# Attention convolutions with taps and channels stacked to 128 rows, their inputs kept as padded maps in DRAM

One core of one Trainium2 chip runs the whole program. The metric is the device time of one execution in microseconds (us); lower is better. The kernel before takes 12191.53 us (median of four runs, 12184.75 to 12194.58).

## The reference, cut to what matters

The program takes four images of 96 channels by 128 x 128 pixels through two layers. The first is a state-space layer (four directional scans). The second, to which the change belongs, splits its normalised input into a positive half x1 and a negative half x2 and runs this on them:

```python
def _relu_split_norm(x, ...):                 # per image: mean, counts, variances, then
    ...                                       # x1 = scale1*relu(x)+shift1 where x>0, else 0 (as built)
    return (out, sc1 * x1 + x1n, sc2 * x2 + x2n)

def _attn_conv(x1, x2, aw1, aw2, aw3):        # C = 96, K = 3, kk = 9, pad = 1
    key = _unfold_nonoverlap(_conv2d(x1, aw1, pad), K).reshape(B, C, kk, -1)
    qry = _unfold_nonoverlap(_conv2d(x2, aw2, pad), K).reshape(B, C, kk, -1)
    attn = jnp.einsum('bckl,bqkl->bqck', key, qry)
    attn = softmax(attn.reshape(B, C, C * kk) / sqrt(C * kk), axis=2)
    w_attn = attn.reshape(B, C, C, K, K)      # a 3x3 convolution kernel for each image
    value = _conv2d(x1, aw3, pad)
    return jax.vmap(lambda v, w: _conv2d(v[None], w, pad)[0])(value, w_attn)

y1 = _layer_norm(_attn_conv(x1, x2, aw1, aw2, aw3))
y2 = _layer_norm(_conv2d(x2, w_conv2, K // 2)) * x1
```

So there are five 3x3 convolutions of 96 to 96 channels for each image: keys and queries (needed only as 3x3 patches), value ("v"), the plain one ("c"), and the last with the softmax weights ("apply").

## The kernel before

An image's normalised input `X` lies in SBUF. Strips of nine rows are made from it, one half at a time, with a border of zeros. Each convolution is nine matmuls with 96 rows, one for a tap, over three image rows (384 columns). Keys and queries are 15 matmuls whose stationary operand is the image (126 patch positions), copied by VectorE to unit step first.

```python
def make_half(dst, src, side, scale, shift):            # ACT scales, DVE masks
    nc.scalar.activation(dst, src, AF.Identity, scale=..., bias=...)
    nc.vector.scalar_tensor_tensor(dst, src, 0.0, dst, ALU.is_le if side else ALU.is_gt, ALU.mult)

def strip(t, side):
    xs = p2.tile([C, 13, W + 2], F32, name="xs")
    # ... memsets of the border ...
    make_half(xs[:, a:e, 1 : W + 1], src, side, scale, shift)      # src: rows of X in SBUF
    x5 = p2.tile([C, 5, 3, 4, NI], F32, name="x5")                 # NI = 42
    by3 = xs[:, 0:12].rearrange("p (i r) w -> p r i w", r=3)
    for sw in range(5):
        nc.vector.tensor_copy(x5[:, sw], by3[:, :, :, sw : sw + 3 * NI - 2 : 3])
    return xs, x5

def unfolded(x5, w, name, bufs):          # 3 groups of 15 matmuls; lhsT = x5[:, sw, ...] (96x126, unit step)
    ...
def conv(xs, w, r, n):
    pc = ps.tile([C, 3, W], F32, name="pc")
    for t in range(KK):                   # KK = 9
        dh, dw = divmod(t, 3)
        nc.tensor.matmul(pc[:, :n], lhsT=w[:, t], rhs=xs[:, r + dh : r + dh + n, dw : dw + W], ...)
    return pc

for t in range(NST):                      # NST = 14 strips of ST = 9 rows
    xs1, x51 = strip(t, 0)
    key = unfolded(x51, ws[0], "key", 2)
    # ... v convolution of the strip into vpad (SBUF, padded) ...
    xs2, x52 = strip(t, 1)
    qry = unfolded(x52, ws[1], "qry", 1)
    # ... key x query matmuls, c convolution to DRAM ...
# attn_apply: 32 chunks of nine matmuls over 512 columns of vpad, weights watT from SBUF
```

In the scan of the first layer, a small input `xr` comes by DMA for every two steps:

```python
def front(n):
    xr = p2.tile([KS, 2 * SN], BF16, name="xr", bufs=3)
    for a, img in enumerate(imgs):
        nc.sync.dma_start(xr[a * KI : (a + 1) * KI], xsp[img][k][:, sl])
    # ... pd = wdt x xr (TensorE), softplus and exp (ACT) ...
```

Of the kernel before, what the change touches and what calls it, by code (L numbers as in the profile page):

```python
# [32 lines left out]
KW = 3 * C  # L33
ROWS = (0, 2, 1, 3)
# [13 lines left out]
def kernel(  # L48
# [67 lines left out]
    def filled(value, name):  # L116
        t = const.tile([C, C], F32, name=name, tag=name)
        nc.vector.memset(t, value)
        return t
# [3 lines left out]
    mean192 = filled(1.0 / (2 * C), "mean192")  # L123
    eps = const.tile([C, 1], F32, name="eps", tag="eps")
# [205 lines left out]
    def ssm_scan(zs, xsp, yms):  # L330
# [6 lines left out]
        with (  # L337
# [26 lines left out]
            def front(n):  # L364
# [6 lines left out]
                xr = p2.tile([KS, 2 * SN], BF16, name="xr", bufs=3)  # L371
# [254 lines left out]
    def attn_maps(p1, X, vpad, scale, shift, c2d):  # L626



        watT = p1.tile([C, KK, C], F32, name="watT")  # L630
        c2st = p1.tile([C, NST * 3 + 1, 6], F32, name="c2st")
        with (
            tc.tile_pool(name="w1", bufs=1) as pw,
            tc.tile_pool(name="d2", bufs=2) as p2,
            tc.tile_pool(name="dps", bufs=2, space=PSUM) as ps,
        ):
            ws = []
            for name, src in (("k", aw1), ("q", aw2), ("v", aw3), ("c", w_conv2)):
                t = pw.tile([C, KK, C], F32, name=f"w_{name}")
                nc.sync.dma_start(t, src)  # L640
                ws.append(t)
            nc.gpsimd.memset(vpad[:, 0 : H + 2 : H + 1, :], 0.0)
            nc.gpsimd.memset(vpad[:, 1 : H + 1, 0 : W + 2 : W + 1], 0.0)


            pa = ps.tile([C, 2, 512], F32, name="pa", bufs=1)

            def strip(t, side):
                r0 = t * ST
                n = 13 if t == NST - 1 else 12  # L650
                xs = p2.tile([C, 13, W + 2], F32, name="xs")
                lo, hi = max(r0 - 1, 0), min(r0 - 1 + n, H)
                a, e = lo - (r0 - 1), hi - (r0 - 1)
                nc.gpsimd.memset(xs[:, :n, 0 : W + 2 : W + 1], 0.0)  # L654
                if a > 0:
                    nc.gpsimd.memset(xs[:, 0], 0.0)
                if e < n:
                    nc.gpsimd.memset(xs[:, e:n], 0.0)
                src = X[:, lo * W : hi * W].rearrange("p (h w) -> p h w", w=W)
                make_half(xs[:, a:e, 1 : W + 1], src, side, scale, shift)  # L660

                x5 = p2.tile([C, 5, 3, 4, NI], F32, name="x5")
                by3 = xs[:, 0:12].rearrange("p (i r) w -> p r i w", r=3)
                for sw in range(5):
                    nc.vector.tensor_copy(x5[:, sw], by3[:, :, :, sw : sw + 3 * NI - 2 : 3])  # L665
                return xs, x5

            def unfolded(x5, w, name, bufs):

                m = p2.tile([3 * NI, KK, C], F32, name=name, bufs=bufs)  # L670
                for kh in range(3):
                    pk = ps.tile([3 * NI, KW], F32, name="pk")
                    order = [(dh, sw) for dh in range(3) for sw in (2, 0, 1, 3, 4)]
                    for n, (dh, sw) in enumerate(order):
                        sh = kh + dh
                        k0, k1 = max(0, sw - 2), min(2, sw)
                        at = dh * 3 + 2 - sw + k0
                        nc.tensor.matmul(  # L678
                            pk[:, k0 * C : (k1 + 1) * C],
                            lhsT=x5[:, sw, sh % 3, sh // 3 : sh // 3 + 3].rearrange(  # L680
                                "p i j -> p (i j)"
                            ),
                            rhs=w[:, at : at + k1 - k0 + 1].rearrange("p t o -> p (t o)"),
                            start=(n == 0),
                            stop=(n == len(order) - 1),
                        )
                    nc.scalar.copy(
                        m[:, kh * 3 : kh * 3 + 3].rearrange("p t o -> p (t o)"), pk
                    )
                return m  # L690

            def conv(xs, w, r, n):
                pc = ps.tile([C, 3, W], F32, name="pc")
                for t in range(KK):
                    dh, dw = divmod(t, 3)
                    nc.tensor.matmul(  # L696
                        pc[:, :n],
                        lhsT=w[:, t],
                        rhs=xs[:, r + dh : r + dh + n, dw : dw + W],
                        start=(t == 0),  # L700
                        stop=(t == KK - 1),
                    )
                return pc

            for t in range(NST):
                chunks = [(0, 3), (3, 3), (6, 3)] + ([(9, 2)] if t == NST - 1 else [])
                xs1, x51 = strip(t, 0)
                key = unfolded(x51, ws[0], "key", 2)
                for r, n in chunks:
                    pc = conv(xs1, ws[2], r, n)  # L710
                    row = t * ST + r + 1
                    nc.vector.tensor_copy(vpad[:, row : row + n, 1 : W + 1], pc[:, :n])  # L712
                xs2, x52 = strip(t, 1)
                qry = unfolded(x52, ws[1], "qry", 1)
                for k in range(KK):
                    nc.tensor.matmul(
                        pa[:, k // 5, (k % 5) * C : (k % 5 + 1) * C],
                        lhsT=qry[:, k],
                        rhs=key[:, k],
                        start=(t == 0 and k in (0, 5)),  # L720
                        stop=(t == NST - 1 and k in (4, 8)),
                    )
                for i, (r, n) in enumerate(chunks):
                    pc = conv(xs2, ws[3], r, n)
                    cc = p2.tile([C, 3 * W], F32, name="cc")
                    nc.scalar.copy(cc[:, : n * W], pc[:, :n].rearrange("p h w -> p (h w)"))  # L726
                    nc.vector.bn_stats(c2st[:, t * 3 + i], cc[:, : n * W])  # L727
                    at = (t * ST + r) * W
                    nc.sync.dma_start(c2d[:, at : at + n * W], cc[:, : n * W])


            sm = p2.tile([C, KK, C], F32, name="sm", tag="qry", bufs=1)
            nc.vector.tensor_copy(
                sm[:, 0:5].rearrange("p t o -> p (t o)"), pa[:, 0, : 5 * C]
            )
            nc.scalar.copy(sm[:, 5:9].rearrange("p t o -> p (t o)"), pa[:, 1, : 4 * C])
            flat = sm.rearrange("p t o -> p (t o)")
            s = 1.0 / math.sqrt(C * KK)
            mx = col("mx")
            nc.vector.reduce_max(mx, flat, AX.X)  # L740
            nc.vector.tensor_scalar(mx, mx, -s, None, ALU.mult)
            den = col("den")
            nc.scalar.activation(flat, flat, AF.Exp, scale=s, bias=mx, accum_out=den)
            nc.vector.reciprocal(den, den)
            nc.vector.tensor_scalar(flat, flat, den, None, ALU.mult)
            for k in range(KK):
                pT = ps.tile([C, KW], F32, name="pk")
                nc.tensor.transpose(pT[:, :C], sm[:, k], ident)
                nc.vector.tensor_copy(watT[:, k], pT[:, :C])  # L749
        return watT, c2st  # L750

    def attn_apply(p1, vpad, watT, od):

        ost = p1.tile([C, NCH, 6], F32, name="ost")
        with (
            tc.tile_pool(name="e3", bufs=3) as p3,
            tc.tile_pool(name="eps", bufs=4, space=PSUM) as ps,
        ):
            for c in range(NCH):
                po = ps.tile([C, R, W], F32, name="poc")  # L760
                for t in range(KK):
                    dh, dw = divmod(t, 3)
                    nc.tensor.matmul(  # L763
                        po,
                        lhsT=watT[:, t],
                        rhs=vpad[:, c * R + dh : c * R + dh + R, dw : dw + W],
                        start=(t == 0),
                        stop=(t == KK - 1),
                    )
                oc = p3.tile([C, CH], F32, name="oc")  # L770
                nc.scalar.copy(oc, po.rearrange("p h w -> p (h w)"))
                nc.vector.bn_stats(ost[:, c], oc)
                nc.sync.dma_start(od[:, bass.ts(c, CH)], oc)
        return ost
# [153 lines left out]
```

## Time and profile before

The stages are read from the first and last record of each kind in the trace: a scan from the first to the last of GpSimd's sums into `y`; the wait from the last coefficient of the split to the first attention matmul; the maps stage from there to the first transpose of the softmax weights; the transition from there to the first apply matmul; apply to its last matmul; the end to the last matmul of the output stage (`pf`). The scan runs twice, the rest four times.

| stage, kernel before | us each | times |
|---|---|---|
| scan | 1047.9 | 2 |
| wait for the first attention matmul | 4.1 | 4 |
| maps (keys, queries, v, c) | 930.9 | 4 |
| transition to apply | 3.2 | 4 |
| apply | 247.4 | 4 |
| end | 166.0 | 4 |

How the page shows that TensorE bounds the maps and apply stages is told in the prediction below, with its lines.

### The profile page before, as it was taken

To read this page: it belongs to the slowest core of one execution; us is meant where nothing else is said; L and a number is where in the kernel's file an instruction comes from. 1 tells how busy PE (TensorE), PEld (TensorE's weight loads), DVE (VectorE), ACT (ScalarE), POOL (GpSimd) and SP (SyncE) were. 2 spreads that over 40 slices of the span, in tenths; PEclk is the share of its full clock that TensorE was granted. 3 is DMA by queue.
4 is the path that set the end of the run, shared out by engine and by line. 5 is a ranking of instruction groups with operands and counts; after the bars stand their busy time and mean duration, and the time that the engine had idled before them with its cause. 6 is when DMAs were issued, how large, how long until landed. Compare 5 with 4: busy or idle time off the path is not lost. (4 is left out here: it accounts for less than half of the span.)

```text
span 12183.9 us, 75678 instructions
## 1 busy us (share of the span) xinstructions
PE 9313.2 (76%) x29184; PEld 4477.1 (37%) x29184; DVE 4792.4 (39%) x4422; ACT 3083.6 (25%) x3474; POOL 2677.1 (22%) x1557
## 2 busy tenths in 40 slices
PE   6949655564999874999879496555649998759998
PEld 2313211112766323775223132111227762236752
DVE  1010088876222375221410101888752213752215
ACT  0000166734111123110200002667331112231102
POOL 1000099940000110000200001999300002100003
PEclk9979855566999876999789797555669998769997
DMA  1030212221000230000210302222300002300003
GB/s 40 27 69 27 67 59 73 83 93 31 8 7 10 64 111 15 8 7 13 87 49 27 71 26 78 62 70 71 99 24 7 8 11 73 108 7 8 8 14 95
DMA packets 256745, 552.66 MB, mean 45 GB/s; under 512 B 69210, under 2 KB 86518, under 8 KB 249216
## 3 DMA queue, kind: packets, MB, share of 16 engines
q1 hardware_dynamic: 231840, 472.09, 13.7%
q0 software_dynamic: 24544, 75.73, 2.1%
q8 instruction: 230, 3.77, 0.1%
q14 instruction: 131, 1.07, 0.0%
HBM read 306.33 MB, written 241.17 MB: 45 GB/s over the span
## 5 line engine op out<-in xcount | busy, mean ns | idle before, releaser
L271 PE MATMUL pz<-xs,weff 97*96 97x512 f32 x4608 | 2018.0, 596 | 14.7 <-DVE xs L256 14.7
L271 PEld LDWEIGHTS pz<-xs,weff 97*96 97x96 f32 x4608 | 741.8, 163 | 1285.7 <-issue 1208.6
L401 PE MATMUL pB<-xr,wbc 60*128 60x512 bf16 (+1 forms) x768 | 387.6, 599 | 1012.1 <-DVE h L439 595.0
L448 POOL TENSOR_TENSOR y<-y,t 128x1024 f32<-128x1024 f32 x384 | 1041.8, 2715 | 61.3 <-DVE t L443 58.5
L419 POOL TENSOR_TENSOR t<-dl,u 128x1024 f32<-128x1024 f32 x384 | 998.0, 2605 | 244.1 <-DMA u<-zs 214.6
L696 PE MATMUL pc<-xs,w_v 96*96 96x384 f32 (+1 forms) x3096 | 1013.5, 487 | 19.0 <-DVE xs L622 19.0
L696 PE MATMUL pc<-xs,w_c 96*96 96x384 f32 (+1 forms) x3096 | 1000.2, 482 | 0.0
L763 PE MATMUL poc<-vpad,watT 96*96 96x512 f32 x2304 | 989.8, 592 | 1.7 <-DVE watT L749 1.7
L678 PE MATMUL pk<-w_k,x 96*126 96x96 f32 (+2 forms) x5040 | 856.4, 334 | 3.0 <-DVE x L665 3.0
L678 PEld LDWEIGHTS pk<-w_k,x 96*126 96x126 f32 x5040 | 795.2, 199 | 84.5 <-issue 8.4
L654 POOL MEMSET xs<- 96x24 f32 (+1 forms) x112 | 14.1, 128 | 3588.9 <-PE pc L696 3313.3
L678 PE MATMUL pk<-w_q,x 96*126 96x96 f32 (+2 forms) x5040 | 801.3, 320 | 0.0
L401 PEld LDWEIGHTS <-wbc 60*128 60x128 bf16 (+1 forms) x1536 | 189.7, 124 | 1649.8 <-issue 1427.0
L678 PEld LDWEIGHTS pk<-w_q,x 96*126 96x126 f32 x5040 | 747.6, 189 | 70.6 <-issue 8.4
L293 DVE COPY xn<-px 32x512 f32<-32x512 f32 x128 | 86.6, 676 | 1717.4 <-PE px L289 1717.4
L278 ACT ACTIVATE z<-pz,dwb 96x512 f32<-96x512 f32 x256 | 174.9, 683 | 2031.6 <-PE pz L271 2031.6
L696 PEld LDWEIGHTS pc<-xs,w_v 96*96 96x96 f32 x3096 | 503.0, 164 | 494.9 <-issue 491.5
L696 PEld LDWEIGHTS pc<-xs,w_c 96*96 96x96 f32 x3096 | 498.4, 162 | 471.3 <-issue 467.2
L712 DVE COPY vpad<-pc 96x384 f32<-96x384 f32 (+1 forms) x172 | 94.8, 551 | 1355.7 <-PE pc L696 1355.7
L727 DVE BATCH_NORM_STATS2 c2st<-cc 96x6 f32<-96x384 f32 (+1 forms) x172 | 95.1, 553 | 1339.9 <-ACT cc L726 1339.9
L424 DVE TENSOR_TENSOR pB<-t,pB 128x1024 f32<-128x1024 f32 x384 | 471.0, 1227 | 361.9 <-POOL t L419 341.6
L328 ACT ACTIVATE dl<-pd,dtb 128x512 f32<-128x512 f32 x768 | 491.9, 684 | 428.1 <-PE pd L380 419.9
(186 smaller groups left out, 10788.4 us busy)
## 6 DMA issues: line engine op xcount, KB each, us to landing
xr<-xsp SPq DMA_DIRECT2D x256, 240.0 KB
zs<-z POOLq DMA_DIRECT2D x128, 384.0 KB, 3.4
u<-zs SPq DMA_DIRECT2D x96, 512.0 KB
yms<-y SPq DMA_DIRECT2D x96, 512.0 KB
yc<-yms SPq DMA_DIRECT2D x128, 384.0 KB
xsp<-piece SPq DMA_DIRECT2D x144, 192.0 KB
xr<-in_x SPq DMA_DIRECT2D x32, 768.0 KB
xc<-in_x SPq DMA_DIRECT2D x128, 192.0 KB
```

Of the source, the lines that this page charges most:

```text
L271: nc.tensor.matmul(pz, lhsT=weff[:, t, j * C : (j + 1) * C], rhs=xs[:, q * R + dh : q * R + dh + R, dw : dw + W], start=(t == 0), stop=(t ...
L278: nc.scalar.activation(z[:, j], pz.rearrange("p h w -> p (h w)"), AF.Silu, bias=dwb[:, j : j + 1],)
L328: nc.scalar.activation(dst, src, AF.Softplus, bias=bias)
L401: nc.tensor.matmul(p[:, j : j + CH], lhsT=wbc[0 : xr.shape[0], steps[n][0], q], rhs=xr[:, j : j + CH], start=True, stop=True,)
L419: nc.gpsimd.tensor_mul(by_rows(t), by_rows(live[n]["dl"]), view(n, 0))
L424: nc.vector.tensor_mul(p, live[n]["t"], p)
L448: nc.gpsimd.tensor_add(yv, yv, by_rows(live[n]["t"]))
L678: nc.tensor.matmul(pk[:, k0 * C : (k1 + 1) * C], lhsT=x5[:, sw, sh % 3, sh // 3 : sh // 3 + 3].rearrange("p i j -> p (i j)"), rhs=w[:, at ...
L696: nc.tensor.matmul(pc[:, :n], lhsT=w[:, t], rhs=xs[:, r + dh : r + dh + n, dw : dw + W], start=(t == 0), stop=(t == KK - 1),)
L712: nc.vector.tensor_copy(vpad[:, row : row + n, 1 : W + 1], pc[:, :n])
L727: nc.vector.bn_stats(c2st[:, t * 3 + i], cc[:, : n * W])
L763: nc.tensor.matmul(po, lhsT=watT[:, t], rhs=vpad[:, c * R + dh : c * R + dh + R, dw : dw + W], start=(t == 0), stop=(t == KK - 1),)
```

## The change

The intent: 96 of 128 rows of the array are used, and a matmul costs the same for 96 rows as for 128. Nine taps of 96 channels are 864 rows, which is six full matmuls of 128 rows and one of 96. A stack puts channels of two rows of the image (different taps) above one another in the partitions. The program makes these stacks by DMA: x1, x2 and the value go to DRAM as padded maps with a pitch of 129 (one zero column serves as right border of a row and left border of the next), and the strips are loaded back stacked.

The diff, cut to its core:

```diff
+PW = W + 1              # pitch 129
+GR = 44                 # image rows are stored grouped by row mod 3, 44 to a group
+GP = 3 * PW + 1
+MAP = 3 * GR * PW + 4
+    zeros = filled(0.0, "zeros", 2 * PW)        # 1 KB a partition, for the whole program
@@ scan
-                xr = p2.tile([KS, 2 * SN], BF16, name="xr", bufs=3)
+                xr = p2.tile([KS, 2 * SN], BF16, name="xr")          # the pool has two buffers
@@ attention
+    def load_strip(pool, m, t):                 # three stacks, 13 DMAs
+        for i, parts in enumerate((
+            ((0, 0, 96, 0, 0), (96, 0, 32, 1, 0)),           # y1: tap row 0, and 32 channels of tap row 1
+            ((0, 32, 96, 1, 0), (64, 0, 64, 2, 0)),          # y2: 64 channels of tap row 1, 64 of tap row 2
+            tuple((32 * d, 64, 96, 2, d) for d in range(3)), # y3: 32 channels of tap row 2, shifted by 0, 1, 2
+        )):
+            y = pool.tile([128 if i < 2 else C, 3, GP], F32, ...)
+            for p, c0, c1, dh, d in parts:
+                for lo, hi, src in groups_of(m, t, dh, d, n):    # one load for rows that lie in several groups
+                    nc.sync.dma_start(y[p : p + c1 - c0, lo:hi, 0:n], src[c0:c1])
+    def store_strip(m, t, y):                   # three DMAs, rows of 129 floats (516 bytes)
+        for r in range(3 if t < NST else 2):
+            ...
+            nc.sync.dma_start(dst, y[:, r : r + 3 * n - 2 : 3])
+    def conv(pc, strip, ws, i, n):              # seven matmuls
+        terms = [(y, w[:, d], d) for d in range(3) for y, w in ((y1, ws[0]), (y2, ws[1]))]
+        terms.append((y3, ws[2], 0))
+        ...
+    def unfolded(ps, m, strip, ws):             # 3 groups of 13 matmuls
+            ...
+                    lhsT=y[:, kh, sw : sw + 382 : 3],            # straight from the strip, step 3 (12 bytes)
-                x5 = p2.tile([C, 5, 3, 4, NI], F32, name="x5")
-                for sw in range(5):
-                    nc.vector.tensor_copy(x5[:, sw], by3[:, :, :, sw : sw + 3 * NI - 2 : 3])
+    def halves_out(p2, X, x1d, x2d, scale, shift):
+        for t in range(NST + 1):
+            for side, m in ((0, x1d), (1, x2d)):
+                y = p2.tile([C, ST, PW], F32, name="half")
+                nc.gpsimd.memset(y[:, :, 0:1], 0.0)
+                make_half(y[:, 0:n, 1:PW], src, side, scale, shift)
+                store_strip(m, t, y)
+    # attn_maps: weights packed to 128 rows by 28 loads, then for each strip
+                s1 = load_strip(p2, x1d, t)
+                ...                                          # keys, v convolution into vt
+                store_strip(vd, t, vt)
+                s2 = load_strip(p2, x2d, t)
+                ...                                          # queries, key x query, c convolution
+            nc.sync.dma_start(watd, watT)                    # softmax weights to DRAM
+    # attn_apply: 7 loads of packed softmax weights, then seven matmuls a chunk of 384 columns from vd
@@ one image
-                watT, c2st = attn_maps(xp, X, vpad, scale, shift, c2d)
-                ost = attn_apply(xp, vpad, watT, od)
+            with tc.tile_pool(name="hv", bufs=3) as p2:
+                halves_out(p2, X, x1d, x2d, scale, shift)    # all 30 halves, ahead of the loop over strips
+            c2st = attn_maps(xp, x1d, x2d, vd, c2d, watd)
+            ost = attn_apply(xp, vd, watd, od)
```

## The prediction

> **What bounds the kernel now.** I first read the busy shares in 40 slices, to see which engine is full in which stage (one digit is a tenth of a slice of 305 us; PEclk is the granted TensorE clock):
>
> ```profile
> PE   6949655564999874999879496555649998759998
> POOL 1000099940000110000200001999300002100003
> PEclk9979855566999876999789797555669998769997
> ```
>
> GpSimd is full only in the two scans. The four runs of 9 on PE, with the clock near full, are the attention of the four images. Then the costliest groups, for the matmuls that the change touches (line, out<-in, count | busy us, mean ns | idle before):
>
> ```profile
> L696 PE MATMUL pc<-xs,w_v 96*96 96x384 f32 (+1 forms) x3096 | 1013.5, 487 | 19.0 <-DVE xs L622 19.0
> L696 PE MATMUL pc<-xs,w_c 96*96 96x384 f32 (+1 forms) x3096 | 1000.2, 482 | 0.0
> L763 PE MATMUL poc<-vpad,watT 96*96 96x512 f32 x2304 | 989.8, 592 | 1.7 <-DVE watT L749 1.7
> L678 PE MATMUL pk<-w_k,x 96*126 96x96 f32 (+2 forms) x5040 | 856.4, 334 | 3.0 <-DVE x L665 3.0
> L678 PE MATMUL pk<-w_q,x 96*126 96x96 f32 (+2 forms) x5040 | 801.3, 320 | 0.0
> ```
>
> Idle time is nearly zero, so PE is the limit of these stages. Each f32 matmul stands as two records (4 images x 43 chunks x 9 taps = 1548, recorded 3096 times). The table by stretches for image 0, maps stage and apply stage, agrees: PE is busy 843 of 847 us and 243 of 245, and DVE, ACT, POOL (the last three busy columns) are far from full:
>
> ```profile
> 2988.00:3835.00 847.00, 842.64 (x3932) 596.46 (x3933) 192.75 (x247) 91.72 (x141) 3.40 (x26) 0.98 0.02 7
> 3930.00:4175.00 245.00, 243.15 (x567) 91.87 (x565) 22.57 (x33) 19.86 (x34) 0.00 (x0) 1.00 0.09 26
> ```
>
> By first and last record, the maps stage lasts 931 us for each image and the apply stage 248 us: 4 x 1179 = 4716 of 12193 us. Matmul records overlap, so their mean is no cost. I took the cost from the evictions, one per finished sum, in the timeline of ACT:
>
> ```profile
> 3192.00 0.47 ACT L726 COPY cc<-pc 96x384 f32<-96x384 f32 x1 [6.94 <-PE pc L696]
> 3197.81 0.47 ACT L726 COPY cc<-pc 96x384 f32<-96x384 f32 x1 [5.33 <-PE pc L696]
> ...
> 3208.31 0.40 ACT L687 COPY key<-pk 126x288 f32<-126x288 f32 x1 [2.65 <-PE pk L678]
> 3213.03 0.40 ACT L687 COPY key<-pk 126x288 f32<-126x288 f32 x1 [4.33 <-PE pk L678]
> ```
>
> A convolution chunk of nine matmuls over 384 columns takes 5.81 us (645 ns each, 1.68 ns a column). A group of fifteen for keys or queries takes 4.72 us. In the same way an apply chunk of nine over 512 columns takes 7.72 us (858 ns each).
>
> For the fifteen I looked at the start of each record: a record of 288 columns takes 243 ns to the next start, 192 columns 163 ns, but 96 columns 109 ns where 82 would follow from its columns. So the short ones are held by their weight load of 126 columns. The rule max(columns x 0.84 ns, 109 ns), on 3x288, 6x192 and 6x96, twice each, gives 2 x (729+978+654) = 4722 ns, the 4.72 us seen.
>
> **What the Trainium skill says.**
> 1. "TensorE: Matmul & The Clock Gate", section "Why this matters for your kernels": a matmul with few rows takes as long as one with 128. The trace agrees: the same pd matmul over 512 columns has mean 618 ns with 60 rows and 620 ns with 120. So 128 rows for 96 should cost nothing.
> 2. Same page, "LDWEIGHTS (loading the stationary operand)": time is columns / 1.2 ns, whatever the rows. 126 columns give 105 ns; the trace shows 109.
> 3. "SBUF — State Buffer", section "Door 1: The DMA port swizzle", on cachelines: lines are 16 bytes, and each crossing to a new line costs unless a line is hit at least twice. The new unfold takes its weights with a step of 3 floats, 12 bytes, where the old one had copied them to step 1. The trace shows such a cost on VectorE (form: minimum/median/maximum ns):
>
> ```profile
> L665 DVE COPY x<-xs x560: 801/830/875, 2992.9 to 11697.5; 96x504 f32<-96x504 f32 x187
> L308 DVE COPY t<-tcol x4: 3646/3658/3665, 719.8 to 7520.8; 64x4096 f32<-64x4096 f32 x4
> ```
>
> Taking off some 155 ns of fixed time (a copy of 384 elements takes 554 ns, 400 at one per 0.96 GHz cycle), L665 costs 675/504 = 1.34 ns an element at step 3. That is three new lines for four elements, 1.79 ns a line. L308 reads at a step of 32 floats, each element a new line, in pairs: 3503/2048 = 1.71 ns. So about 1.75 ns per new line. For TensorE's weight reads no record of this kernel shows it: every f32 weight load has step 1. If the same holds there (estimate), 128 columns at step 3 take 128 x 0.75 x 1.75 = 168 ns and not 111.
> 4. "DMA: Bandwidth & Descriptors", "Anatomy of one DMA — SWDGE (gpsimd) path": about 2 us of fixed time per DMA. The trace has 3.1 to 3.4 us from issue to landing for the 192 and 384 KB stores on that queue.
>
> **The change part by part.**
> - *Convolutions v and c.* Seven for nine: 42 chunks x (9-7) x 645 ns, and one short chunk x 2 x 432 ns = 55 us an image for each of the two; x 8 = **-440 us**.
> - *Apply.* Before 32 x 7.72 = 247 us; after 42 chunks x 7 x 645 ns + 3.0 = 193 us. 4 x 54 = **-217 us**.
> - *Keys and queries.* Thirteen matmuls: two of 288 columns, four of 192, seven of 96. If a weight load takes 168 ns, the 288s cost 243 ns and the others 168: 2 x (486 + 11x168) = 4.67 us for 4.72, x 84 groups x 4 images = **-20 us**. If step 3 is free, 2 x (486 + 4x163 + 7x111) = 3.83 us and -300 us.
> - *The x5 copies* (429 us of DVE) go, but DVE was idle beside PE: 0.
> - *Halves through DRAM.* Before, PE starts 3.5 us after the coefficients (ACT at 2988.2, first convolution 2991.7). Now 30 half strips are each scaled (ACT about 1.3 us), masked (DVE 1.3), stored by three DMAs and loaded again. Strip 0 needs the first two strips of x1: about 7 us of compute, 3.5 of landing, then 13 loads. SP takes some 0.45 us from issue to issue, shown below, so these take 6 us and 3 more to land, among stores of the same queue with three buffers (a buffer's round about 7.5 us, so 2.5 us a half, 75 us for all). I put the start at 35 us: +31 an image, **+125 us**. The rest of the halves lies beside PE work.
> - *Strip loads.* 13 DMAs, 1.6 MB in 1056 runs of 1552 bytes: 66 runs for each of 16 engines, at 66 to 105 ns (the packets of 1536 bytes in this trace), 4.4 to 6.9 us. With issue and landing some 9 to 10 us. Two buffers, and a strip keeps PE 13.5 us in apply (3 x 4.5) and some 25 in maps: hidden, if the issues run ahead of the stores. The scheduler does let them: in the timeline of the SP queue a load of od is issued before the last store to it.
>
> ```profile
> 4173.23 0.30 SPq L794 DMA_DIRECT2D o<-od  x1
> 4173.79 0.30 SPq L773 DMA_DIRECT2D od<-oc  x1
> 4174.15 0.42 SPq L796 DMA_DIRECT2D c<-c2d  x1
> 4174.66 0.41 SPq L798 DMA_DIRECT2D xnc<-xnew  x1
> ```
>
>   I allow **+30 us** for waits that remain.
> - *Softmax weights through DRAM* before apply: a store and seven loads, 3 + 3 + 3 us: **+36 us** over four images.
> - *Zeros of six maps* at the start: 24 small DMAs x 0.45 us: **+10 us**.
> - *xr with two buffers for three in the scan.* A load then waits for the last use two steps later, 11.9 us. At 2000 us the first matmul of a load issued at 1999.8 starts at 2005.2, its product is used by GpSimd at 2020.5 though ready at 2008.9: 11.6 us of slack, against a matmul that moves from 2005.2 to about 2013.7. Hidden, but the margin is thin: **+15 us**.
>
> Sum: 12193 - 440 - 217 - 20 + 125 + 30 + 36 + 10 + 15 = 11732. With step 3 free it is 11452. I give the free case a quarter: 0.75 x 11732 + 0.25 x 11452 = 11662.
>
> **The rivals.**
> 1. *The weight load pays nothing for step 3.* For: weights come at one element in 0.83 ns, slower than DVE's port has to be fed, so the lines may be buffered. Against: 1.75 ns per line on DVE is a time of the memory. Time 11450.
> 2. *It pays more*, a full line for each element (220 ns or over): a group takes 2 x (486 + 11x220) = 5.8 us, +1.1 x 336 = +365 us, total about 12100: no gain.
> 3. *PE waits for the strips.* One queue issues everything; if loads stand behind stores that wait for evictions, each of the 45 strips an image shows some 9 us: 4 x 45 x 9 = +1600 us and a slower kernel. The order above speaks against it. A partial form, all halves stored before the first load, would add 4 x 50 = 200 us.
> 4. *The clock falls* because more rows work. The granted clock is 0.98 to 1.00 in these stages now; nothing on this page shows it depends on rows.
>
> **Range and chances.** Rivals 1 and 2 span 11450 to 12100, rival 3 in part shifts by 200. Low 11400, high 11960. Faster by over 2% means under 11949: 0.88; within 2%: 0.09; slower: 0.03.
>
> **What would show it.** Convolution evictions 4.5 us apart in maps and apply, at clock 1.00 (the row claim). Group evictions of keys about 4.7 us apart, or 3.8 if step 3 is free, with weight-load starts 168 or 111 ns apart. First convolution some 35 us after the coefficients. PE idle before its strips near zero within a stage. Scan steps still 5.97 us. The prediction is wrong if the conv chunks are not 4.5 us, if the group is above 5 us, or if PE waits for DMA in every strip.

## The result, and the profile after

The kernel after takes **12193.96 us** (median of four runs, 12190.1 to 12194.91), against 12191.53 us before. The ratio is 1.0002, with a 95% interval of 0.9985 to 1.0019: the same. A ratio in this document is the mean time of one kernel's fast runs over that of the other's in the same rounds, so it is not quite the ratio of the medians that stand beside it. The prediction was wrong: 11662, with a range of 11400 to 11960.

The stages, read as before:

| stage | before, us | after, us | times | change in all, us | predicted, us |
|---|---|---|---|---|---|
| scan | 1047.9 | 1127.0 | 2 | +158 | +15 |
| wait for the first attention matmul | 4.1 | 121.6 | 4 | +470 | +125 |
| maps and transition | 934.2 | 828.6 | 4 | -422 | -394 |
| apply | 247.4 | 197.4 | 4 | -200 | -217 |
| end | 166.0 | 169.0 | 4 | +12 | 0 |
| all else (profiled spans 12183.9 and 12192.7, less the above) | | | | -9 | +10 |
| sum | | | | +9 | -461 |

The maps row of the prediction is -440 (v and c), -20 (keys and queries), +30 (strip waits) and +36 (softmax weights). So these two rows gave 622 us, where 611 were promised, and two other stages took it back. The page of the kernel after, in 40 slices (a digit is a tenth of a slice of 305 us; PEclk is the granted TensorE clock):

```profile
PE   6949654454599872899879495444546998719998
POOL 1000098860000120000200001988600001200002
PEclk9979855556799875999789797555667998759997
```

Against the lines of before, the four slices of the first scan read 9 8 8 6 on POOL where they read 9 9 9 4: the same work, less dense and longer. The second scan shows the same. The costliest groups of the kernel after answer to those of before:

```profile
L733 PE MATMUL pk<-w_k,y 128*128 128x96 f32 (+2 forms) x3360 | 666.1, 354 | 489.2 <-DMA y<-x1d 489.1
L710 PE MATMUL poc<-y,wat 128*96 128x384 f32 (+1 forms) x2064 | 689.7, 486 | 39.0 <-DMA y<-vd 39.0
L710 PE MATMUL pc<-y,w_v 128*96 128x384 f32 (+1 forms) x2064 | 690.6, 482 | 0.0
```

The last field of a line is idle time just before the group. Before, it was 3.0 us for the key groups; now it is 489 us, nearly all of it spent on a DMA of a strip of x1. The value convolution has none, and by the timeline nearly all of this idle time falls at four places, 120 to 125 us once for each image:

```profile
3181.11 5.93 PE L733 MATMUL pk<-w_k,y 128*128 128x288 f32 x20 [120.85 <-DMA y<-x1d]
```

**The convolutions.** The evictions of finished sums, in the timeline of DVE, are one for a chunk of seven matmuls:

```profile
3202.29 0.55 DVE L797 COPY vt<-pc 96x384 f32<-96x384 f32 x1 [43.26 <-PE pc L710]
3206.82 0.56 DVE L797 COPY vt<-pc 96x384 f32<-96x384 f32 x1 [3.98 <-PE pc L710]
```

They lie 4.53 us apart, where nine matmuls took 5.81: the ratio is 0.780, and 7/9 is 0.778. The granted clock in the maps stage is 1.00 and in apply 0.99. (The mean of the whole run fell from 0.819 to 0.791: some 620 us of matmuls at a clock near 1.00 gave way to as much time in the wait and the scan, where the tables by stretches show 0.50.)

**Keys.** The evictions of key groups, in the timeline of ACT:

```profile
3188.12 0.50 ACT L740 ACTIVATE key<-pk,patches 128x288 f32<-128x288 f32 x1 [29.55 <-PE pk L733]
3192.94 0.50 ACT L740 ACTIVATE key<-pk,patches 128x288 f32<-128x288 f32 x1 [4.32 <-PE pk L733]
```

A group of thirteen takes 4.82 us; fifteen took 4.72 before, and 4.67 was predicted. With the prediction's own formula, 2 x (486 + 11 x L) = 4820 ns, a weight load L takes 175 ns. The records agree: the weight loads of the 96-column matmuls `pk<-w_kr` start 174 ns apart (median).

**The wait.** The timeline of the SP queue (what SP issues) around the last stores of image 0's halves:

```profile
3100.31 1.34 SPq L701 DMA_DIRECT2D x2d<-half  x3
3101.70 0.49 SPq L691 DMA_DIRECT2D y<-x1d  x1
...
3159.09 0.77 SPq L701 DMA_DIRECT2D x2d<-half  x2
3159.90 3.32 SPq L691 DMA_DIRECT2D y<-x1d  x2
3163.83 0.32 SPq L671 DMA_DIRECT2D w_k<-in_aw  x1
...
3178.43 2.66 SPq L691 DMA_DIRECT2D y<-x1d  x5
```

Stores of halves (`x2d<-half`) run from 3064.4 to 3159.9 us. A few loads of strips stand among them, but the rest come only after the last store, and between those and the last five stand 28 loads of packed weights, from 3163.8 to 3178.4. The first matmul is at 3181.11. Sizes tell which loads go early: the six of x1 are four of 48.5 KB and two of 97, just those of the thirteen that take a single row, and all seven that take two or three rows are late. So three things share the wait: the stores themselves, the strip loads that come only after all of them, and the weights in the queue ahead. How busy the DMA engines were is in the table by stretches for 3064 to 3160 (busy time of PE, PEld, DVE, ACT, POOL, then the clock, the mean busy share of the 16 DMA engines, and GB/s):

```profile
3064.00:3160.00 96.00, 0.00 (x0) 0.00 (x0) 37.64 (x30) 36.35 (x29) 2.96 (x27) 0.50 0.94 137
```

DVE and ACT are busy little over a third of the time, and the DMA engines 0.94 of it, at only 137 GB/s. In the view of DMA for the same stretch, 26,284 packets take 93.5% of 16 engines: 0.935 x 16 x 96 us / 26,284 = 55 ns a packet, most of them rows of 516 bytes.

**The scan.** The timeline of GpSimd at 2000 us, kernel after and then kernel before:

```profile
2007.01 3.09 POOL L458 TENSOR_TENSOR y<-y,t 128x1024 f32<-128x1024 f32 x1 [1.93 <-DVE t L453]
2010.06 5.67 POOL L429 TENSOR_TENSOR t<-dl,u 128x1024 f32<-128x1024 f32 x2
2015.69 3.06 POOL L458 TENSOR_TENSOR y<-y,t 128x1024 f32<-128x1024 f32 x1
2020.71 3.13 POOL L458 TENSOR_TENSOR y<-y,t 128x1024 f32<-128x1024 f32 x1 [1.95 <-DVE t L453]
```

```profile
2002.59 2.86 POOL L419 TENSOR_TENSOR t<-dl,u 128x1024 f32<-128x1024 f32 x1
2005.41 3.07 POOL L448 TENSOR_TENSOR y<-y,t 128x1024 f32<-128x1024 f32 x1
2008.56 2.87 POOL L419 TENSOR_TENSOR t<-dl,u 128x1024 f32<-128x1024 f32 x1
```

Before, GpSimd alternated t and y without a gap. After, it runs t, t, y, y, and waits 1.9 us for DVE ahead of the second y; DVE in turn waits 2.5 us for a t. A pair of steps takes 20.71 - 7.01 = 13.70 us from one such wait to the next; before, it took 11.96.

Two things narrow this down. Some 70 of the 79 us lie in the middle third of the scan and some ten steps before it: of its 192 steps, 64 to 127 take 79 to 95 us for each sixteen before and 96 to 110 after; in the outer thirds, with the same two buffers, GpSimd mostly alternates and sixteen steps take at most some 5 us more. And the order t, t, y, y on GpSimd is not the loss by itself. The kernel before runs it too in places, without a gap (steps 81 and 82, 11.70 us):

```profile
1952.18 5.68 POOL L419 TENSOR_TENSOR t<-dl,u 128x1024 f32<-128x1024 f32 x2
1957.80 6.14 POOL L448 TENSOR_TENSOR y<-y,t 128x1024 f32<-128x1024 f32 x2
```

The kernel after takes 13.68 us for the same two steps. One difference there is the order on VectorE: before, it runs a product (`pB<-t,pB`), the scan (`h`) and a second product (`t<-h,pC`) for one step and then for the next; after, it runs the first product of both steps before either scan, and GpSimd's second y waits for the last of the six.

**Apply.** Its first chunk waits for the first strip of the value, once an image:

```profile
4009.15 10.13 PE L710 MATMUL poc<-y,wat 128*96 128x384 f32 x22 [9.87 <-DMA y<-vd]
```

The rest of the 18 us between the first transpose and apply is the nine transposes and the last c convolution, which the scheduler put behind them.

### The profile page after: what moved, and what is told of

It is laid out like the page before. It is cut to its first block, busy times and chain, and to the rows that moved or that the text cites. A ratio compares the mean times of both kernels' runs of the same rounds, so it can differ in the third digit from the quotient of the medians.

```text
span 12192.7 us, 75341 instructions
## 1 busy us (share of the span) xinstructions
PE 8685.5 (71%) x26568; PEld 4373.1 (36%) x26568; DVE 4403.2 (36%) x4024; ACT 3106.7 (25%) x3522; POOL 2666.5 (22%) x1601
## 3 DMA queue, kind: packets, MB, share of 16 engines
q14 instruction: 163, 1.34, 0.0%
## 5 line engine op out<-in xcount | busy, mean ns | idle before, releaser
L733 PE MATMUL pk<-w_k,y 128*128 128x96 f32 (+2 forms) x3360 | 666.1, 354 | 489.2 <-DMA y<-x1d 489.1
L733 PEld LDWEIGHTS pk<-w_k,y 128*128 128x128 f32 x3360 | 656.9, 261 | 506.1 <-issue 500.0
L710 PE MATMUL poc<-y,wat 128*96 128x384 f32 (+1 forms) x2064 | 689.7, 486 | 39.0 <-DMA y<-vd 39.0
L710 PE MATMUL pc<-y,w_c 128*96 128x384 f32 (+1 forms) x2064 | 696.1, 485 | 2.5 <-DMA y<-x2d 1.8
L710 PE MATMUL pc<-y,w_v 128*96 128x384 f32 (+1 forms) x2064 | 690.6, 482 | 0.0
L733 PEld LDWEIGHTS pk<-w_q,y 128*128 128x128 f32 x3360 | 652.1, 260 | 13.2 <-issue 9.1
L733 PE MATMUL pk<-w_q,y 128*128 128x96 f32 (+2 forms) x3360 | 656.1, 351 | 0.0
L294 POOL DMA_DIRECT2D zs<-z x128 | 96.2, 751 | 2140.5 <-ACT z L288 1701.9
L411 PE MATMUL pC<-xr,wbc 60*128 60x512 bf16 (+1 forms) x768 | 410.3, 611 | 191.8 <-DVE t L453 191.8
L513 DVE RECIPROCAL sd<-sd 96x512 f32<-96x512 f32 x128 | 419.9, 3320 | 287.5 <-ACT sd L512 287.5
```

Source lines behind the costliest of these rows:

```text
L294: nc.gpsimd.dma_start(zs[:, row * W : row * W + CH].rearrange("(j p) l -> p j l", j=2), z)
L411: nc.tensor.matmul(p[:, j : j + CH], lhsT=wbc[0 : xr.shape[0], steps[n][0], q], rhs=xr[:, j : j + CH], start=True, stop=True,)
L513: nc.vector.reciprocal(sd, sd)
L710: nc.tensor.matmul(pc[:, :n], lhsT=w, rhs=y[:, 0:n, o : o + W], start=(at == 0), stop=(at == len(terms) - 1),)
L733: nc.tensor.matmul(pk[:, k0 * C : k1 * C], lhsT=y[:, kh, sw : sw + 382 : 3], rhs=w.rearrange("p t o -> p (t o)"), start=(i == 0), stop=(i ...
```

## The experiments

Theory at the outset: the gain of the matmuls is real and was given back in two places, the scan (two buffers for `xr`) and the wait for the halves (all stored ahead of the loop); the step of 3 takes a further part away. Rivals were that the scan was slow for other reasons (DMA traffic of the new maps), that the wait is one of transfer or issue whatever the order, and that the step costs nothing so that the group is held by something else. All kernels gave the right result unless it is said otherwise.

### xr3: the scan's third buffer back

The constant `zeros` goes into a pool that is closed at once, which makes room.

```diff
-                xr = p2.tile([KS, 2 * SN], BF16, name="xr")
+                xr = p2.tile([KS, 2 * SN], BF16, name="xr", bufs=3)
-    zeros = filled(0.0, "zeros", 2 * PW)
+    with tc.tile_pool(name="z0", bufs=1) as z0:
+        zeros = z0.tile([C, 2 * PW], F32, name="zeros")
```

> The changed kernel with three xr buffers in the scan again (the row of zeros moves to a short-lived pool to make room). Theory: the two scans became 79 us longer each (1048 to 1127 us from first to last GpSimd addition) only because an xr load now waits two steps longer; so both return to 1048 us and the time falls by 158 us to about 12035 us. Rival: the scan is longer because the scheduler ordered it otherwise for another reason (maps, constants); then it stays at 1127 us and the time at 12190.

Measured: 12052.4 us, ratio to before 0.9885 (0.9868 to 0.9901). The scan takes 1049 us, all other stages stand as in the kernel after (wait 121, maps 810). At 2000 us GpSimd alternates again, without gaps.

### before_xr2: the same edit in the kernel before

```diff
-                xr = p2.tile([KS, 2 * SN], BF16, name="xr", bufs=3)
+                xr = p2.tile([KS, 2 * SN], BF16, name="xr")
```

> The kernel before with two xr buffers for three and nothing else. Theory: its scans go from 1048 to about 1127 us each and the time from 12192 to about 12350 us. Rival (the slack of 11.6 us read from the trace hides it, and something else made the scan longer): 12190 to 12210 us.

Measured: 12347.74 us against 12190.06, ratio 1.0127 (1.0112 to 1.0142); the scan takes 1127 us with no attention map in sight, and a pair of steps at 2000 us the same 13.70 us, in the same order. The buffer count alone makes the loss, +79 us a scan; the traffic of the maps has no part in it.

### unit_step: the keys' and queries' weights read at step 1 (a wrong result)

```diff
-                    lhsT=y[:, kh, sw : sw + 382 : 3],
+                    lhsT=y[:, kh, sw : sw + 128],
```

> The changed kernel with the weights of the key and query groups read at step 1 instead of step 3 from the same strips (wrong result on purpose). Theory: step 3 is what makes a weight load of 128 columns cost some 175 ns; at step 1 it costs about 111 ns, a group of thirteen falls from 4.82 to 3.83 us, and 336 groups save 333 us: about 11860 us. Rival (the loads are slow for their 128 columns or for the order of the thirteen): group and time unchanged, about 12190 us.

Measured: 11871.37 us, ratio 0.9737 (0.9722 to 0.9751). The maps stage falls from 810.4 to 729.5 us. Two consecutive evictions of key groups:

```profile
3195.54 0.50 ACT L740 ACTIVATE key<-pk,patches 128x288 f32<-128x288 f32 x1 [3.33 <-PE pk L733]
3199.38 0.50 ACT L740 ACTIVATE key<-pk,patches 128x288 f32<-128x288 f32 x1 [3.33 <-PE pk L733]
```

A group takes 3.84 us; the prediction's case of a free step had 3.83. The same matmuls with the same operands but for the step cost 0.98 us less, and 0.98 x 84 groups = 82 us an image, which is the 81 us of the stage.

### step4: the same at 16 bytes (wrong on purpose, one look)

```diff
-                    lhsT=y[:, kh, sw : sw + 382 : 3],
+                    lhsT=y.rearrange("p r x -> p (r x)")[:, kh * 300 + sw : kh * 300 + sw + 127 * 4 + 1 : 4],
```

> The changed kernel with the weights of the key and query groups read at step 4, that is 16 bytes, each element in a line of its own (wrong result on purpose). If a weight load costs a fixed time for each new 16-byte line (175 ns at step 3 is 1.78 ns for each of 96 lines), step 4 makes it 128 x 1.78 + 4 = 232 ns, a group 2 x (2x243 + 11x232) = 6.08 us for 4.82 and the time about 12610 us. Rival: any step but 1 costs the same 175 ns: 12190.

Measured: 12576.54 us (one run, state unknown); the maps stage takes 917 us. A group is (917 - 810.4) / 84 = 1.27 us longer than at step 3, so 6.09 us, or L = 233 ns. Now 128 columns touch 32 lines of 16 bytes at step 1, 96 at step 3 and 128 at step 4. Step 3: 175 / 96 = 1.82 ns a line; step 4: 233 / 128 = 1.82 ns a line. At step 1, 32 lines would take 58 ns, and L is the 111 ns of the columns. The starts of the weight loads `pk<-w_kr` show the same without the formula: 112, 174 and 233 ns apart (medians of unit_step, the kernel after and step4). So the three points fit the larger of two times, that of the columns and that of the lines. They do not show that lines are what counts: up to step 4 the lines grow with the stretch of memory that is spanned (32, 96 and 128 lines for 512, 1536 and 2048 bytes), and no run has a larger step, which would tell the two apart.

### deinterleaved: one copy for each strip tile, right result

```diff
+        for i, y in enumerate(strip):
+            z = pool.tile([y.shape[0], 3, 3, PW], F32, name=f"z{i}", tag=f"z{i}")
+            nc.vector.tensor_copy(z, y[:, :, 0 : 3 * PW].rearrange("p r (j s) -> p s r j", s=3))
-                    lhsT=y[:, kh, sw : sw + 382 : 3],
+                    lhsT=y[:, sw % 3, kh, sw // 3 : sw // 3 + 128],
```

> The changed kernel with each strip copied once by VectorE into three planes (column modulo 3), so that the key and query groups read their weights at step 1 and the result is right. Theory: a group falls to 3.83 us as in unit_step, the three copies of a strip (1161 elements at step 3 each, about 1.7 us) hide beside PE; about 11870 us. Rival: the copies delay the first group of each strip, or VectorE holds up the evictions, and half of the gain is lost: about 12030.

Measured: 11839.3 us, ratio 0.9715 (0.9701 to 0.973). The maps stage takes 730 us, as in unit_step: three copies by DVE for a strip (where the kernel before made five) buy the unit step back, and lie wholly beside TensorE. The wait also fell, from 121.6 to 112 us, because the last store comes 90 us after the coefficients and not 98; why the stores run faster there, no run shows.

### lazy_halves: the halves stored two strips ahead, inside the loop

```diff
-    def halves_out(p2, X, x1d, x2d, scale, shift):
-        for t in range(NST + 1):
+    def halves_out(p2, X, x1d, x2d, scale, shift, ts):
+        for t in ts:
...
+            halves_out(ph, *hv, range(2))
             for t in range(NST + 1):
...
                 store_strip(vd, t, vt)
+                halves_out(ph, *hv, range(t + 2, min(t + 3, NST + 1)))
```

> The changed kernel with the halves of strips 0 and 1 stored before the maps loop and those of strip t+2 inside it, behind the value convolution of strip t. Theory: PE waits some 117 us an image for strip 0 because its loads stand in the SP queue behind the stores of all thirty halves and the 28 weight loads; now the first attention matmul comes about 35 us after the coefficients instead of 120, four times 85 = 340 us less, about 11855 us. Rival (the SP queue or DMA transfer itself is the limit, so the waits move into the loop): PE then idles in front of later strips and the time falls by less than 100 us.

Measured: 11842.63 us, ratio 0.9713 (0.9699 to 0.9728). The wait falls from 121.6 to 32.8 us an image, and the maps stage stays at 810 us: the stores of the later halves lie beside TensorE's work. In the lists of waits of PE, the kernel after and then this one (total us, times, longest):

```profile
PE pk L733 <- DMA y<-x1d: 489.1, 6, 124.8
```

```profile
PE pk L733 <- DMA y<-x1d: 133.7, 4, 33.8
```

The prediction had put the start at 35 us, from "the first two strips". That sum was right for a kernel that stores two strips first, which the kernel after is not.

### weights_early: the 28 packed weights loaded before the output of the first layer

```diff
+            ws = load_weights(xp)
             ssm_output(b, yms, X, stats, xnew)
```

> The changed kernel with the 28 packed weight loads issued before the SSM output stage, and nothing else. Theory: the wait of 120 us for strip 0 is mostly the stores of the halves ahead in the SP queue, and the weights only stand in the last 15 us of it (issued from 103 to 118 us after the coefficients); so the wait falls to about 107 us and the time by some 50 us to about 12140. Rival: the weights are the cause; then the wait falls to about 35 us and the time to about 11850.

Measured: 12132.4 us, ratio 0.9957 (0.994 to 0.9974). The wait is 96 us, 25 less, where 107 was expected. The queue of SP shows both parts: no weights stand between the last store and the last strip loads (some 15 us), and with no early strip loads among them the stores run from 3080.7 to 3166.0, in 85 us and not 95.

### halves_apart, halves_apart_rows, halves_apart_six: why the strips don't start early

These three carry weights_early and ask what keeps the first strip until after the last store. In the kernel after, the pool of the halves is closed before the strips' pool opens, so the strips may lie in its memory. halves_apart keeps it open:

```diff
             with tc.tile_pool(name="hv", bufs=3) as p2:
                 halves_out(p2, X, x1d, x2d, scale, shift)
-            c2st = attn_maps(xp, x1d, x2d, vd, c2d, watd)
+                c2st = attn_maps(xp, ws, x1d, x2d, vd, c2d, watd)
```

> The changed kernel with weights early and the pool of the halves kept open over the attention, so that no strip or weight tile takes the memory of a half; all halves still before the loop. Weights early alone left a wait of 96 us. Rival: strip tiles wait for the memory of the halves; then the wait falls to about 40 us. Theory: a load of several rows spans, in its hull, parts of the map that later strips store, and is held until the last store; only loads of one row go early. Then the wait stays at 95 us, the single-row loads come within 40 us of the coefficients and the others only after the last store.

Measured: 12178.9 us beside 12187.85 of before (one run each, state unknown). The wait is 108 us, so the start does not hang on shared memory. (It is 12 us longer than in weights_early: early loads stand among the stores again, and these take 98 us and not 85.) The SP queue:

```profile
3133.02 0.49 SPq L691 DMA_DIRECT2D y<-x2d  x1
...
3178.86 0.78 SPq L701 DMA_DIRECT2D x2d<-half  x2
3179.68 4.40 SPq L691 DMA_DIRECT2D y<-x1d  x7
```

In this timeline the loads that go early are those of one row group (0.49 us to issue, `x1`; six of x1's thirteen, of the same sizes as in the kernel after), and those that span two or three row groups of the map come after the last store. Single rows do not always go early: in weights_early and halves_apart_six none of the thirteen does, and no run shows what decides that. My reading: rows are stored grouped by row mod 3, so the span from the first to the last element of a load over two groups covers rows that later stores still write, and the load is ordered behind all of them. The next kernel cuts every strip load to single row groups (21 for a strip):

```diff
-                if at + n <= GR * PW:
+                if hi - lo == 1 and at + n <= GR * PW:
```

> As halves_apart, with every strip load cut into loads of one row (21 for 13), so that none is held by a later store. If the hull is all that holds them, strip 0 is loaded within 60 us. If the slots of the SP queue between the stores hold them then (in its order two or three loads stand between each two groups of stores, the last behind the last store), the wait stays near 95 us. I expect the latter, with some 10 us on top in apply for the longer issue at most.

Measured: 12147.64 us (one run). The first matmul now comes 29 us after the coefficients and not 108, so with the pool kept open the form of the loads was what held the first strip. (Single rows without the open pool were not tried.) But the maps stage grew to 880 us: wait and maps together take 909 us, 9 less than halves_apart and 3 more than weights_early. TensorE starts early and then waits for each next load, 221 us in 13 waits over the run, since the loads are issued one after another among the stores. The order of issue and the transfers may stand behind the ordering as the next limit; that was not tested apart.

The last asks whether three buffers hold the stores back, as the prediction thought (a buffer's round of 7.5 us):

```diff
-            with tc.tile_pool(name="hv", bufs=3) as p2:
+            with tc.tile_pool(name="hv", bufs=6) as p2:
```

> As halves_apart, with six buffers for the halves instead of three. If the round of a buffer (scale, mask, three stores, landing) sets the 3.3 us between halves, it falls to the 1.4 us of ACT, DVE or three issues, all thirty are stored in some 45 us and the wait falls from 95 to about 55 us. If the DMA transfer of 516-byte rows is the limit, it stays above 85.

Measured: 12176.1 us (one run), wait 106 us: the buffers are not the limit. The same table by stretches, with six buffers:

```profile
3075.00:3170.00 95.00, 0.00 (x0) 0.00 (x0) 36.99 (x29) 35.63 (x28) 2.63 (x24) 0.50 1.15 133
```

The rate is 133 GB/s for 137 (and for 133 at a share of 0.98 in halves_apart, 3079 to 3178). With more stores in flight each packet takes longer (the busy share rises to 1.15; above 1 it means that packets of one engine overlap in the records), and no more bytes pass. That the transfer holds the stores is the likely reading, but 137 GB/s is no fixed ceiling: weights_early, with three buffers and no early loads among the stores, moves 148 (3081 to 3166).

### all_mended: all of it

xr3, lazy_halves, weights_early and deinterleaved together, and the first value strip of apply loaded ahead of the softmax weights.

```diff
+            st = load_strip(p2, vd, 0)
             w1, w2, wr, last = packed_weights(pw, watd, "wat")
...
-                st = load_strip(p2, vd, t)
+                st = st if t == 0 else load_strip(p2, vd, t)
```

> The changed kernel with three xr buffers, halves stored two strips ahead inside the loop, weights loaded early, strips copied into planes for keys and queries, and strip 0 of the value loaded before the packed softmax weights. If the causes are separate and add up: 12194 - 142 (xr) - 351 (halves) - 322 (step) - 20 (start of apply) = about 11360 us. Rival: the queue of SP or VectorE becomes the limit of the maps loop when both are mended; then the maps stage stays above 740 us an image and the time above 11450.

Measured: **11373.81 us** (11365.43 to 11383.02, four fast runs), correct, ratio 0.9333 (0.9319 to 0.9347): faster than both kernels by 6.7%. Scan 1048, wait 23.6, maps 729.5, transition 17, apply 198. Two lines of its list of waits stand against the 489 us of the kernel after:

```profile
PE pk L740 <- DMA y<-x1d: 72.9, 3, 24.7
PE pk L740 <- DVE z L724: 23.9, 1, 23.9
```

What remains is one start of some 24 us for each image. The early load of the value strip gained only about 1 us in the transition.

## Why the prediction was wrong, by its own steps

- **Convolutions v and c, and the row claim: right.** 4.53 us for a chunk, predicted 7 x 645 = 4.52; the clock held (rival 4 fell).
- **Apply: nearly right.** -200 for -217; the stage takes 197.4 us for 193.
- **Keys and queries: right in mechanism, a small term mis-sized.** The weight load took 175 ns at step 3 for the 168 worked out from VectorE, which makes a group 4.82 us and not 4.67: 0.10 x 336 = +34 us where -20 stood. unit_step and step4 show that the step is the cause. Rival 1 (a free step, 3.83 us a group) is thus refuted for the kernel as it stands, and the quarter that I gave it pulled the point forecast from 11732 to 11662. What I said for it was also the wrong way round: a weight load of 126 columns in 109 ns, 0.87 ns an element, is faster, not slower, than VectorE's 1.03 (copies of 384 and 256 columns, 554 and 422 ns; their difference gives that and a fixed time of 158 ns, near the 155 that I took off). That 168 came so near is in part luck. Of the two readings behind it, L665 stands: deinterleaved's copies at step 3 take 1735 ns for 1161 elements, 1.36 ns each for its 1.34. L308 does not: 3503 ns for 4096 elements, each on a new line, are 0.86 ns a line, and no line shows the "pairs" that made 1.71 of it. Taking away the copies of VectorE was counted as 0 because VectorE was idle beside TensorE. That was right for VectorE; what they did for TensorE stood in the weight-load term, and the deinterleaved kernel shows its size: 81 us an image.
- **Strip loads and softmax weights: nearly right.** No wait for strips shows in the maps stage outside its start, for +30 allowed; the start of apply waits 9.9 us, for 9. These make up for the keys: maps and transition are -422 for -394.
- **Halves through DRAM: the first failed step.** "Strip 0 needs the first two strips of x1 ... I put the start at 35 us: +31 an image, +125 us" measured 121.6 us, +470. The program stores all 30 halves before the loop, and I assumed that the first loads would pass the stores. The lines that I took this from ("The scheduler does let them") show a load of `od`, one stretch of columns, and not a load over several row groups. halves_apart_rows shows that such loads don't pass; weights_early shows 25 us for the 28 weights in the queue and the loads among the stores; and the size of "2.5 us a half, 75 us for all" was short too: 3.3 us a half were measured (95.4 us from the first store to the last, 29 steps), and six buffers do not shorten it (94 us). Rival 3's partial form, "all halves stored before the first load", was in effect what happened (all seven loads over several rows came after the last store); I gave it 200 us, and the excess over the +125 was 345. lazy_halves, where only two strips go first, measures 32.8 us: the sum was right for a program that this was not.
- **xr with two buffers: the second failed step.** "Hidden, but the margin is thin: +15 us" measured +158. I read 11.6 us of slack from a fixed order of GpSimd's work and asked whether a later load fits in it. With two buffers the scheduler laid the instructions of GpSimd and VectorE in another order, in which they wait for each other in turn. The slack belonged to the old order. xr3 and before_xr2 show the 79 us a scan from both sides. A later load is not what TensorE waits for: its waits for `xr` are 42 us in all, and 47 in the kernel before. That the order makes the loss is still my reading of the timelines; no run holds the order and changes the buffers.

Against the sum of 11732, a change of -461, the profiles show +9: 470 us more. The two failed steps make 345 + 143 = 488 of it, and all others together -18.

## What to carry to other kernels

A gain on the bounding engine is only kept if the work that feeds it is laid into its loop: store or prepare one or two strips ahead, not all ahead of the first load, and look at what stands in the same DMA queue between the last producer and the first consumer. A buffer taken from a stage that the change does not touch is part of the change: where one engine runs without a gap, measure that stage by itself before calling its slack enough. If an operand is read at a step, count the 16-byte lines that it touches (1.82 ns each fits the weight loads here); a copy to unit step on an idle engine may be the cheaper way.

## What the Trainium skill lacked or had wrong

- "SBUF — State Buffer", section "Door 1: The DMA port swizzle": the note on cachelines has no figure, and gives "4 fp32" as how far one can stride for free, though it also wants two hits on a line. The runs show TensorE's weight loads of 128 floats at 111 ns at step 1, 175 at step 3 (12 bytes) and 233 at step 4: steps of 3 and of 4 floats are not free. 1.82 ns for each 16-byte line fits both.
- "TensorE: Matmul & The Clock Gate", section "LDWEIGHTS (loading the stationary operand)": columns / 1.2 ns holds at step 1 (107 for the 111 ns seen) and says nothing of the step, which made 175 of it.
- "DMA: Bandwidth & Descriptors", section "Specifications": at least 512 bytes are given as the transfer for line rate. Rows of 516 bytes in a burst of stores filled the engines (share 0.94) at 137 GB/s, 55 ns a packet, and at 133 GB/s with twice the buffers. By the fit of the section "Anatomy of one DMA — SWDGE (gpsimd) path", which is for another queue, bytes / 436 GB/s would give 30 us (an estimate) for the 13.2 MB that took 96. So rows just over 512 bytes were not enough here; no run varies their length or start, so why stays open.
- No page tells how a load over several row groups of a DRAM tensor is ordered behind stores to other rows of it (first matmul at 108 us with such loads, at 29 with single rows), nor that the number of buffers changes the order of the instructions on the engines (11.96 to 13.70 us for a pair of scan steps).
